# Separate PSUM tiles for the narrow channel group, and layer-norm statistics in three TensorE passes, in a Swin block with a dynamic convolution

## The chip, the cores and the metric

The kernel runs on one NeuronCore of a Trainium2 chip (trn2). The metric is device time in microseconds of one execution, the median of several. The engines are named as in the profile: PE (TensorE) multiplies, PEld loads its weights, DVE (VectorE) and ACT (ScalarE) work on vectors, POOL (GpSimd) works in this kernel on data in SBUF, SP issues transfers. In this kernel PSUM, in banks, holds the results of TensorE; a PSUM tile is what the program allocates there at once, one bank or two. All runs told of here are fast ones; a program on one core shows no second state in these runs.

## The reference, cut to what matters

The input is (16, 192, 56, 56) in f32. One shifted-window attention block (7x7 windows, 6 heads), its MLP, and then a depthwise convolution whose weights depend on the image's pooled result:

```python
h = _ln(transpose(x), norm1_g, norm1_b)          # over 192 channels
...                                              # roll, windows, attention
x1 = shortcut + transpose(h)
y = _ln(transpose(x1), norm2_g, norm2_b)         # over 192 channels
y = gelu(y @ fc1_w + fc1_b) @ fc2_w + fc2_b      # 192 -> 768 -> 192
x = x1 + transpose(y)
pooled = x.mean(axis=(2, 3))                     # "taps": weights per image and channel
wt = (relu(bn(pooled @ w1.T)) @ w2.T + b2) * MASK
out = depthwise_conv(x, wt) + bias
```

## The kernel before

192 channels are a wide group of 128 and a narrow group of 64. A step handles two rows of windows, 2 x 392 tokens; four steps make an image, 64 steps the batch. The wide group lies on 128 partitions with the two token halves side by side; the narrow group has its two halves one above the other, on partitions 0-63 and 64-127. Each step of the loop carries the MLP of step i-2, the attention of step i, the value and query products of step i+1, the norm-1 statistics of step i+2 and the norm-2 statistics of step i-1, and pieces of an older image's convolution. PSUM is cut into four pairs of banks, called A, B_, C, D in the loop; a pair is one tile.

The statistics are sums over channels of x and of x squared, made by TensorE with a 32-column constant, so that each result lands on one strip of 32 partitions:

```python
def norm_squares(key, i, side, engine):          # engine: ACT for norm 2, GpSimd for norm 1
    ...                                          # s0 = squares of the wide group, s1 of the narrow one
    sqs[key] = s0, s1

def norm_stats(key, i, side):                    # called once for each side
    v0, v1 = flat_of(i)
    s0, s1 = sqs.pop(key)
    st = bank(side)
    for k in range(2):
        for h in range(2):
            for at, u0, u1 in ((side * 64, v0, v1), ((1 - side) * 64, s0, s1)):
                lhs, rhs = (sel[:, 0], u0[:, h]) if k == 0 else (sel[:, 1 + h], u1)
                p = at + h * 32
                mm(st[p : p + 32, :T], lhs, rhs, k == 0, k == 1)
```

The second half of a step, with the two banks of one pair C shared by three narrow results:

```python
singles[0] = banks(f"s_{i}", C)                  # one PSUM tile of two banks
o = attention_rows(i, attention_values(i, prts, D))   # wide into D, narrow into bank(1); ACT copies out
mlp_narrow(hid, bank(0))                         # narrow part of the second MLP product
for c in ys:
    conv_rest(*c)                                # DVE: three taps of a convolution piece
mlp_out(i - 2, 1, bank(0)[:, :T])                # DVE reads bank(0)
pp, pp1, p_narrow, p_rest, p_whole = project(i, o, A)  # wide into A, narrow into bank(1)
p_narrow(); p_rest()
pvs, v_rest, v_whole = attention_v(i + 1, (B_, D))
v_rest()
if (i - 2) % STEPS == STEPS - 1:                 # every fourth step
    convs.append({... "wt": taps(b, taps_pool(b))})    # a small matmul into bank(0), DVE work
p_whole()
residual(i, pp, pp1)                             # DVE
v_whole()
attention_v_out(pvs)                             # DVE and ACT copy the values out
norm_squares(f"2_{i}", i, 1, nc.scalar)          # ACT
```

(Cut: conditions that only matter at the ends of the loop.)

Of the kernel before, what the change touches and what calls it, by code (L numbers as in the profile page):

```python
# [10 lines left out]
ALU = mybir.AluOpType  # L11
# [25 lines left out]
def tile_swin_then_dynamic_conv(  # L37
# [45 lines left out]
    def banks(name, k):  # L83
        return psum.tile([128, 2, 512], F32, tag=f"pair{k}", name=name)
# [3 lines left out]
    def bank(k):  # L88
        return singles[0][:, k]

    def mm(dst, lhs, rhs, start, stop):
        nc.tensor.matmul(dst, lhs, rhs, start=start, stop=stop, skip_group_check=True)  # L92
# [134 lines left out]
    def flat_of(i):  # L227
        v0, v1 = rows_of(i)
        return v0.rearrange("p h r c -> p h (r c)"), v1.rearrange("p r c -> p (r c)")
# [8 lines left out]
    def norm_squares(key, i, side, engine):  # L238
        v0, v1 = flat_of(i)
        s0 = one.tile([128, 2, T], F32, tag=f"sq0{side}", name=f"sq0_{key}")  # L240
        s1 = one.tile([128, T], F32, tag=f"sq1{side}", name=f"sq1_{key}")
        if engine is nc.scalar:
            nc.scalar.activation(s0, v0, AF.Square)
            nc.scalar.activation(s1, v1, AF.Square)
        else:
            engine.tensor_tensor(s0, v0, v0, ALU.mult)
            engine.tensor_tensor(s1, v1, v1, ALU.mult)
        sqs[key] = s0, s1

    def norm_stats(key, i, side):  # L250


        v0, v1 = flat_of(i)
        s0, s1 = sqs.pop(key)
        st = bank(side)
        for k in range(2):
            for h in range(2):
                for at, u0, u1 in ((side * 64, v0, v1), ((1 - side) * 64, s0, s1)):
                    lhs, rhs = (sel[:, 0], u0[:, h]) if k == 0 else (sel[:, 1 + h], u1)
                    p = at + h * 32  # L260
                    mm(st[p : p + 32, :T], lhs, rhs, k == 0, k == 1)
        stats[side] = st

    def norm_vars(keys):

# [243 lines left out]
    def attention_weigh(po, po1, wp, prt):  # L509
        for s in range(2):  # L510
            w = wp * 2 + s
            for a, g in ((0, 0), (0, 1), (1, 0), (1, 1), (0, 2), (1, 2)):

                r, k = (g, a) if g < 2 else (a, 2)
                o = po[:, a] if g < 2 else po1
                at = (g if g < 2 else a) * 64
                mm(
                    o[at : at + 64, w * N : (w + 1) * N],
                    vbd[:, a, w, g, :],
                    prt[:, r, k * PW + s * 64 : k * PW + s * 64 + N],  # L520
                    True,
                    True,
                )

    def attention_values(i, prts, k):

        po = banks(f"po_{i}", k)
        for wp in range(4):
            attention_weigh(po, bank(1), wp, prts[wp])
        return po[:, 0], po[:, 1], bank(1)  # L530

    def attention_rows(i, pos):

# [5 lines left out]
            )  # L539
        return o.rearrange("p k r w c -> p k (r w c)")  # L540

    def project(i, o, k):

        pp = banks(f"pp_{i}", k)
        pp1 = bank(1)

        def narrow():
            for a in range(2):
                mm(pp1[a * 64 : a * 64 + 64, :T], wp0[:, C0:DIM], o[:, a], True, False)

        def rest():
            for a in range(2):
                p = slice(a * 64, a * 64 + 64)
                mm(pp[:, a, :T], wp1[p], o[p, 2], True, False)

        def whole():
            mm(pp1[:, :T], wp2, o[:, 2], False, True)
            for a in range(2):
                mm(pp[:, a, :T], wp0[:, 0:C0], o[:, a], False, True)

        return pp, pp1, narrow, rest, whole
# [39 lines left out]
            long(dsts[f], wf1, cols(f), y0, False)  # L601
            gelu(f)

    def mlp_narrow(hid, pf1):
        for f in range(NFC):
            for a in range(2):
                mm(
                    pf1[a * 64 : a * 64 + 64, :T],
                    wf2[:, f, C0:DIM],
                    hid[:, f, a],  # L610
                    f == 0,
                    f == NFC - 1,
                )

    def mlp_wide(i, hid, k, turn):
        pf = banks(f"pf_{i}", k)
# [8 lines left out]
    def mlp_out(i, c, p):  # L625

        b, s = divmod(i, STEPS)
        if b not in sums:
            sums[b] = small.tile([128, 2, STEPS], F32, tag="sums", name=f"sums_{b}")
        v = flat_of(i)[c]  # L630
        nc.vector.scalar_tensor_tensor(
            v, p, f2b[c], v, ALU.add, ALU.add, accum_out=sums[b][:, c, s : s + 1]
        )
# [8 lines left out]
        nc.vector.tensor_copy(x1[64:128, 0, :], x1[0:64, HALF, :])  # L642
        return pooled

    def taps(b, pooled):

        pt = bank(0)
        for kc in range(2):
            mm(pt[:, 0:RED], pooled[:, kc].broadcast_to([128, 128]), w1t[:, kc], kc == 0, kc == 1)
        tt = small.tile([128, 1, RED], F32, tag="tt", name=f"tt_{b}", bufs=1)  # L650
        nc.vector.tensor_tensor(tt[:, 0], pt[:, 0:RED], bn[:, 0], ALU.mult)
        nc.vector.tensor_tensor(tt[:, 0], tt[:, 0], bn[:, 1], ALU.add)
        tw = small.tile([128, 2 * NTAP, RED], F32, tag="tw", name=f"tw_{b}", bufs=1)
        nc.vector.scalar_tensor_tensor(
            tw,
            tt.broadcast_to([128, 2 * NTAP, RED]),
            0.0,
            w2n.rearrange("p k t r -> p (k t) r"),
            ALU.max,
            ALU.mult,  # L660
        )
        wt = small.tile([128, 2, NTAP], F32, tag="wt", name=f"wt_{b}")
        nc.vector.tensor_reduce(
            wt.rearrange("p k (t o) -> p (k t) o", o=1), tw, AX.X, ALU.add
        )
        nc.vector.tensor_tensor(wt, wt, b2t, ALU.add)
        return wt
# [51 lines left out]
    def has(i):  # L719
        return 0 <= i < NS  # L720
# [11 lines left out]
        return ready  # L732

    def stats_of(i):
        keys = {}
        if has(i + 2):
            keys[0] = f"1_{i + 2}"
            norm_stats(keys[0], i + 2, 0)
        if has(i - 1):
            keys[1] = f"2_{i - 1}"  # L740
            norm_stats(keys[1], i - 1, 1)
        return keys

    def tail_of(i, o, kp, kv):

        pvs, v_rest, v_whole = attention_v(i + 1, kv) if has(i + 1) else (None, None, None)
        if o is not None:
            pp, pp1, narrow, rest, whole = project(i, o, kp)
            narrow()
            rest()  # L750
        if pvs:
            v_rest()
        if o is not None:
            whole()
            residual(i, pp, pp1)
        if pvs:
            v_whole()
            attention_v_out(pvs)
        if o is not None:
            norm_squares(f"2_{i}", i, 1, nc.scalar)  # L760
# [178 lines left out]
    for i, extra in ((0, (proj_bias, mlp_weights)), (1, (taps_weights,))):  # L939
        top, share = attention_scores(i, *qs.pop(i), (1, 2, 0, 1))  # L940
        norm1_scale(i + 1, dvs.pop(0), nc.gpsimd)
        top(0)
        for wp in range(3):
            top(wp + 1)
            share(wp)
        share(3)
        qs[i + 1], outs = attention_qk(i + 1, 1, 0, 2)
        for f in outs:
            f()
        for e in extra:  # L950
            e()
        keys = stats_of(i)
        dev = norm_devs(keys)
        dvs.update(norm_spread(keys, dev))
        prts = [attention_turn(i, wp, wp % 2) for wp in range(4)]
        if 1 in keys:
            yns[i - 1] = norm2_scale(i - 1, dvs.pop(1))
        norm_squares(f"1_{i + 3}", i + 3, 0, nc.gpsimd)
        o = attention_rows(i, attention_values(i, prts, 0))
        tail_of(i, o, 1, (2, 0))  # L960


# [3 lines left out]
    for i in range(2, NS + 2):  # L966
# [67 lines left out]
            yns[i - 1] = norm2_scale(i - 1, dvs.pop(1))  # L1034
        if has(i + 3):
            norm_squares(f"1_{i + 3}", i + 3, 0, nc.gpsimd)
        singles[0] = banks(f"s_{i}", C)
        if has(i):
            o = attention_rows(i, attention_values(i, prts, D))
        mlp_narrow(hid, bank(0))  # L1040
        for c in ys:
            conv_rest(*c)
        mlp_out(i - 2, 1, bank(0)[:, :T])
        if has(i):
            pp, pp1, p_narrow, p_rest, p_whole = project(i, o, A)
            p_narrow()
            p_rest()
        if has(i + 1):
            pvs, v_rest, v_whole = attention_v(i + 1, (B_, D))
            v_rest()  # L1050
        if (i - 2) % STEPS == STEPS - 1:
            b = (i - 2) // STEPS
            convs.append({"b": b, "n": 0, "wt": taps(b, taps_pool(b))})
        if has(i):
            p_whole()
            residual(i, pp, pp1)
        if has(i + 1):
            v_whole()
            attention_v_out(pvs)
        if has(i):  # L1060
            norm_squares(f"2_{i}", i, 1, nc.scalar)
        pairs = [C, A, B_, D]
    c = convs.pop()
    for n in range(6):
        conv_rest(c["b"], c["wt"], n, conv_begin(c["b"], c["wt"], n))
# [74 lines left out]
```

## Time and profile before

| | before |
|---|---|
| median time | 3428.9 us (3428.0 to 3432.4, three runs) |
| TensorE busy | 93% |
| period of a normal step, start of the statistics to the next | 51.06 us |
| period of a step with taps, every fourth | 51.85 us |
| statistics matmuls of one step | 2.84 us |
| granted TensorE clock, 300 to 3000 us | 1.00 |

The periods are the distance between the first statistics matmuls of successive steps in the timeline of TensorE. From the fifth on, all but one repeat within 0.05 us, which makes them a far finer ruler than the total. The length of the statistics is given either to the modelled end of the last matmul (2.84 us before, 2.18 after) or to the start of the next product (2.77 and 2.11). The rows of the page, of the waits and of the timeline are shown in the prediction. In a row of the timeline the bracket is the idle time before an instruction and what ended it; in a row of the waits the three numbers are the total, the count and the longest.

### The profile page before, as it was taken

The numbers are of one execution on the slowest core, as the hardware profiler recorded it, in microseconds if no ns is written. First come the engines' busy times: TensorE is split into PE (matmuls) and PEld (weight loads), VectorE is DVE, ScalarE is ACT, GpSimd is POOL, SyncE is SP. The second block draws the span as 40 slices with busy tenths as digits, with TensorE's granted clock in tenths as the row PEclk, the third lists the DMA queues.
The fourth block names the chain that finished last, engine by engine and source line by source line (L and its number), as shares of the span: only waits on it lengthen the run. The fifth ranks groups of instructions, "written<-read, shape, count | busy, mean of one in ns | idle before, by whom it ended". The sixth has DMA issues, their size and how long they took to land.

```text
span 3430.2 us, 64894 instructions
## 1 busy us (share of the span) xinstructions
PE 3183.9 (93%) x26642; PEld 1955.5 (57%) x26642; DVE 2078.5 (61%) x3893; ACT 1854.5 (54%) x2988; POOL 759.8 (22%) x656
## 2 busy tenths in 40 slices
PE   5799999999999999999999999999999999999996
PEld 3455555555555555555555555555555555555553
DVE  4354675665665665665665666665665656666564
ACT  3354564565565565565565565565565565555552
POOL 4211212212212212212212212212212222222220
PEclk7799999999999999999999999999999999999998
DMA  3101102111111102101111201102111110201001
GB/s 94 19 10 48 29 25 57 34 48 34 51 27 38 53 26 61 29 27 55 34 51 31 59 23 35 53 29 58 29 30 52 34 54 28 62 22 32 25 29 43
DMA packets 79124, 135.39 MB, mean 39 GB/s; under 512 B 21766, under 2 KB 61692, under 8 KB 76908
## 3 DMA queue, kind: packets, MB, share of 16 engines
q1 hardware_dynamic: 77266, 128.54, 13.3%
q8 instruction: 210, 3.44, 0.4%
q0 software_dynamic: 1056, 1.92, 0.3%
q10 hardware_dynamic: 506, 0.79, 0.1%
q14 instruction: 86, 0.70, 0.1%
HBM read 41.25 MB, written 38.54 MB: 23 GB/s over the span
## 4 chain that ended last, share of the span: by engine, by line
PE 84%; ACT 7%; DVE 4%; issue 1%; POOL 0%; DMA 0%; SPq 0%; DVEq 0%; POOLq 0%; ACTq 0%
PE ph L92 23%; PE pf L92 15%; PE s L92 10%; PE pv L92 7%; PE st L92 5%; PE pq L92 4%; PE pp L92 4%; PE sc L92 4%; PE pe L92 4%; PE pk L92 4%; PE pt L500 3%; ACT o L536 2%; ACT prt L506 2%; ACT L235 2%; DVE y L688 2%
## 5 line engine op out<-in xcount | busy, mean ns | idle before, releaser
L92 PE MATMUL ph<-yn,wf 128*128 128x392 f32 (+1 forms) x3072 | 802.3, 498 | 6.1 <-ACT vbd L443 3.3
L487 POOL TENSOR_TENSOR prob<-e,tot 113x588 f32<-113x588 f32 x256 | 297.8, 1174 | 1966.6 <-DVE tot L486 1966.6
L92 PEld LDWEIGHTS ph<-yn,wf 128*128 128x128 f32 (+1 forms) x3072 | 429.4, 189 | 350.6 <-issue 87.2
L443 ACT COPY vbd<-pv 49x192 f32<-49x192 f32 x512 | 135.4, 312 | 888.7 <-DVE vbd L441 888.5
L92 PE MATMUL pf<-hid,wf 128*128 128x392 f32 x1536 | 538.3, 494 | 3.5 <-ACT hid L588 2.0
L688 DVE SCALAR_TENSOR_TENSOR y<-x,wt,y 128x770 f32<-128x770 f32 x288 | 328.1, 1141 | 288.1 <-ACT y L673 281.4
L588 ACT ACTIVATE hid<-ph,f1b 128x784 f32<-128x784 f32 x384 | 336.8, 912 | 137.7 <-PE ph L92 137.7
L92 PEld LDWEIGHTS pf<-hid,wf 128*128 128x128 f32 x1536 | 281.5, 190 | 183.7 <-ACT hid L588 3.3
L92 PE MATMUL s<-hid,wf 128*64 128x392 f32 x1536 | 266.9, 496 | 88.6 <-ACT o L536 88.6
L92 PEld LDWEIGHTS pv<-wqkv,win 64*128 64x128 f32 (+1 forms) x2048 | 259.7, 190 | 39.6 <-ACT kbd L393 2.8
L471 DVE TENSOR_TENSOR e<-sc,bias_t 113x588 f32<-113x588 f32 x256 | 179.5, 761 | 168.0 <-PE sc L92 167.8
L92 PE MATMUL pv<-wqkv,win 64*128 64x192 f32 (+1 forms) x2048 | 274.0, 327 | 3.3 <-ACT kbd L393 2.5
L478 DVE TENSOR_TENSOR e<-e,top 113x588 f32<-113x588 f32 x256 | 266.5, 1041 | 8.9
L338 POOL TENSOR_TENSOR yn<-x,dv 128x784 f32<-128x784 f32 x64 | 132.0, 2063 | 565.4 <-DMA dv<-dev 537.8
L235 ACT ACT_TABLE_LOAD x192 | 246.3, 1283 | 3.4
L506 ACT COPY prt<-pt 128x678 f32<-128x678 f32 x256 | 179.1, 726 | 117.5 <-PE pt L500 116.0
L481 ACT ACTIVATE e<-e 113x588 f32<-113x588 f32 x256 | 176.8, 691 | 108.7 <-DVE e L478 108.7
L92 PEld LDWEIGHTS s<-hid,wf 128*64 128x64 f32 x1536 | 104.5, 137 | 216.2 <-issue 119.9
L441 DVE COPY vbd<-pv 49x192 f32<-49x192 f32 x512 | 159.1, 349 | 97.0 <-ACT vbd L443 83.0
L500 PEld LDWEIGHTS pt<-ident,prob 113*128 113x128 f32 x1536 | 167.3, 142 | 74.4 <-issue 45.3
L500 PE MATMUL pt<-ident,prob 113*128 113x113 f32 x1536 | 182.7, 262 | 10.3 <-ACT prt L506 8.5
L92 PE MATMUL po<-prt,vbd 128*64 128x49 f32 x4096 | 191.5, 225 | 0.2 <-ACT prt L506 0.2
(157 smaller groups left out, 4688.9 us busy)
## 6 DMA issues: line engine op xcount, KB each, us to landing
dv<-dev SPq DMA_DIRECT2D x1020, 49.0 KB
x<-in_x_dram SPq DMA_DIRECT2D x15, 1484.0 KB
out_dram<-y SPq DMA_DIRECT2D x48, 392.0 KB
out_dram<-y SPq DMA_DIRECT2D x48, 196.0 KB
x<-in_x_dram SPq DMA_DIRECT2D x16, 392.0 KB
x<-in_x_dram SPq DMA_DIRECT2D x15, 350.0 KB
out_dram<-y SPq DMA_DIRECT2D x16, 308.0 KB
out_dram<-y SPq DMA_DIRECT2D x16, 154.0 KB
```

The costliest lines, as they stand in the source:

```text
L92: nc.tensor.matmul(dst, lhs, rhs, start=start, stop=stop, skip_group_check=True)
L235: nc.scalar.activation(junk, eps_t[0:1], func)
L441: nc.vector.tensor_copy(dst, f)
L443: nc.scalar.copy(dst, f)
L471: nc.vector.tensor_tensor(e, sc[:PW, :, : HEADS * N], rel, ALU.add)
L478: nc.vector.tensor_tensor(ehs[wp], ehs[wp], t.broadcast_to([PW, 2 * HEADS, N]), ALU.subtract)
L481: nc.scalar.activation(es[wp], es[wp], AF.Exp)
L487: nc.gpsimd.tensor_tensor(prob[wp][:PW, :, 0:N], ehs[wp], t.broadcast_to([PW, 2 * HEADS, N]), ALU.mult)
L500: nc.tensor.transpose(pt[:, a, g * PW : (g + 1) * PW], prob[wp][:PW, h : h + 2, :].rearrange("p h k -> p (h k)"), ident[:PW, :PW],)
L506: nc.scalar.copy(prt, pt[:, :, : 3 * PW])
L588: nc.scalar.activation(hid[:, f], phs[f][:, :, :T], AF.Gelu, bias=f1b[:, f : f + 1])
L688: nc.vector.scalar_tensor_tensor(dst, src, wt[:, kc, t : t + 1], dst, ALU.mult, ALU.add)
```

## The change

It has two aims. First, three statistics passes instead of four: the squares of the narrow group are added to those of the wide group on GpSimd, so that one pass over the sum does what two did, and both sides are run together to keep all four strips of 32 columns full. Second, each narrow result gets a PSUM tile of its own, which needs another turn of the pairs, and the taps move behind the rest of the projection and values to find a free pair.

```diff
+        for h in range(2):
+            p = slice(h * 64, h * 64 + 64)
+            nc.gpsimd.tensor_tensor(s0[p, h], s0[p, h], s1[p], ALU.add)
+        sqs[key] = s0
...
+        for k in range(3):
+            for side in keys:
+                v0, v1 = flat_of(steps[side])
+                for h in range(2):
+                    p = (side if k < 2 else 1 - side) * 64 + h * 32
+                    dst = stats[side][p : p + 32, :T]
+                    if k == 0:
+                        mm(dst, sel[:, 0], v0[:, h], True, False)
+                    elif k == 1:
+                        mm(dst, sel[:, 1 + h], v1, False, True)
+                    else:
+                        mm(dst, sel[:, 0], sqs[keys[side]][:, h], True, True)
...
-        singles[0] = banks(f"s_{i}", C)
-            o = attention_rows(i, attention_values(i, prts, D))
-        mlp_narrow(hid, bank(0))
+            o = attention_rows(i, attention_values(i, prts, D, C))
+        pf1 = mlp_narrow(i - 2, hid, A)
...
-            pp, pp1, p_narrow, p_rest, p_whole = project(i, o, A)
+            pp, pp1, p_narrow, p_rest, p_whole = project(i, o, B_, C)
-            pvs, v_rest, v_whole = attention_v(i + 1, (B_, D))
+            pvs, v_rest, v_whole = attention_v(i + 1, (D, A))
             v_rest()
-        if (i - 2) % STEPS == STEPS - 1:
-            convs.append({"b": b, "n": 0, "wt": taps(b, taps_pool(b))})
             p_whole()
             residual(i, pp, pp1)
             v_whole()
+        if (i - 2) % STEPS == STEPS - 1:
+            convs.append({"b": b, "n": 0, "wt": taps(b, taps_pool(b), C)})
             attention_v_out(pvs)
...
-        pairs = [C, A, B_, D]
+        pairs = [C, B_, D, A]
```

(Cut: the first two steps, the signatures, conditions that only matter at the ends.)

More of the change, by code (lines that the diff above doesn't have):

```diff
@@ L247, in norm_squares, with norm_stats @@
             engine.tensor_tensor(s1, v1, v1, ALU.mult)
-        sqs[key] = s0, s1
-    def norm_stats(key, i, side):
-        v0, v1 = flat_of(i)
-        s0, s1 = sqs.pop(key)
-        st = bank(side)
-        for k in range(2):
-            for h in range(2):
-                for at, u0, u1 in ((side * 64, v0, v1), ((1 - side) * 64, s0, s1)):
-                    lhs, rhs = (sel[:, 0], u0[:, h]) if k == 0 else (sel[:, 1 + h], u1)
-                    p = at + h * 32
-                    mm(st[p : p + 32, :T], lhs, rhs, k == 0, k == 1)
-        stats[side] = st
+        for h in range(2):
+            p = slice(h * 64, h * 64 + 64)
+            nc.gpsimd.tensor_tensor(s0[p, h], s0[p, h], s1[p], ALU.add)
+        sqs[key] = s0
+    def norm_stats(keys, steps):
+        for side in keys:
+            stats[side] = bank(side)
+        for k in range(3):
+            for side in keys:
+                v0, v1 = flat_of(steps[side])
[8 more added lines that the diff above has]
+                        mm(dst, sel[:, 0], sqs[keys[side]][:, h], True, True)
+        for side in keys:
+            sqs.pop(keys[side])
     def norm_vars(keys):
@@ L523, in attention_weigh, with attention_values @@
                 )
-    def attention_values(i, prts, k):
-        po = banks(f"po_{i}", k)
+    def attention_values(i, prts, k, k1):
+        po, po1 = banks(f"po_{i}", k), banks(f"po1_{i}", k1)[:, 0]
         for wp in range(4):
-            attention_weigh(po, bank(1), wp, prts[wp])
-        return po[:, 0], po[:, 1], bank(1)
+            attention_weigh(po, po1, wp, prts[wp])
+        return po[:, 0], po[:, 1], po1
     def attention_rows(i, pos):
@@ L540, in attention_rows, with project @@
         return o.rearrange("p k r w c -> p k (r w c)")
-    def project(i, o, k):
-        pp = banks(f"pp_{i}", k)
-        pp1 = bank(1)
+    def project(i, o, k, k1):
+        pp, pp1 = banks(f"pp_{i}", k), banks(f"pp1_{i}", k1)[:, 0]
         def narrow():
@@ L602, in mlp_first, with mlp_narrow @@
             gelu(f)
-    def mlp_narrow(hid, pf1):
+    def mlp_narrow(i, hid, k):
+        pf1 = banks(f"pf1_{i}", k)[:, 0]
         for f in range(NFC):
@@ L613, in mlp_narrow @@
                 )
+        return pf1
     def mlp_wide(i, hid, k, turn):
@@ L643, in taps_pool, with taps @@
         return pooled
-    def taps(b, pooled):
-        pt = bank(0)
+    def taps(b, pooled, k):
+        pt = banks(f"t_{b}", k)[:, 0]
         for kc in range(2):
@@ L734, in stats_of @@
     def stats_of(i):
-        keys = {}
-        if has(i + 2):
-            keys[0] = f"1_{i + 2}"
-            norm_stats(keys[0], i + 2, 0)
-        if has(i - 1):
-            keys[1] = f"2_{i - 1}"
-            norm_stats(keys[1], i - 1, 1)
+        steps = {side: k for side, k in ((0, i + 2), (1, i - 1)) if has(k)}
+        keys = {side: f"{side + 1}_{k}" for side, k in steps.items()}
+        norm_stats(keys, steps)
         return keys
@@ L747, in tail_of @@
         if o is not None:
-            pp, pp1, narrow, rest, whole = project(i, o, kp)
+            pp, pp1, narrow, rest, whole = project(i, o, kp, 3)
             narrow()
@@ L949, in tile_swin_then_dynamic_conv @@
             f()
+        if i:
+            singles[0] = banks("singles", 3)
         for e in extra:
@@ L958, in tile_swin_then_dynamic_conv @@
         norm_squares(f"1_{i + 3}", i + 3, 0, nc.gpsimd)
-        o = attention_rows(i, attention_values(i, prts, 0))
+        o = attention_rows(i, attention_values(i, prts, 0, 3))
+        singles[0] = None
         tail_of(i, o, 1, (2, 0))
@@ L1036, in tile_swin_then_dynamic_conv @@
             norm_squares(f"1_{i + 3}", i + 3, 0, nc.gpsimd)
-        singles[0] = banks(f"s_{i}", C)
         if has(i):
-            o = attention_rows(i, attention_values(i, prts, D))
-        mlp_narrow(hid, bank(0))
+            o = attention_rows(i, attention_values(i, prts, D, C))
+        pf1 = mlp_narrow(i - 2, hid, A)
         for c in ys:
             conv_rest(*c)
-        mlp_out(i - 2, 1, bank(0)[:, :T])
+        mlp_out(i - 2, 1, pf1[:, :T])
         if has(i):
-            pp, pp1, p_narrow, p_rest, p_whole = project(i, o, A)
+            pp, pp1, p_narrow, p_rest, p_whole = project(i, o, B_, C)
             p_narrow()
@@ L1048, in tile_swin_then_dynamic_conv @@
         if has(i + 1):
-            pvs, v_rest, v_whole = attention_v(i + 1, (B_, D))
+            pvs, v_rest, v_whole = attention_v(i + 1, (D, A))
             v_rest()
-        if (i - 2) % STEPS == STEPS - 1:
-            b = (i - 2) // STEPS
-            convs.append({"b": b, "n": 0, "wt": taps(b, taps_pool(b))})
         if has(i):
@@ L1058, in tile_swin_then_dynamic_conv @@
             v_whole()
+        if (i - 2) % STEPS == STEPS - 1:
+            b = (i - 2) // STEPS
+            convs.append({"b": b, "n": 0, "wt": taps(b, taps_pool(b), C)})
+        if has(i + 1):
             attention_v_out(pvs)
```

## The prediction

> **What bounds the kernel now.** I read the page first (busy times and the clock row), then the list of waits, then one step in order of time on each engine. The page says that TensorE is busy for 93% of the span, and no other engine for more than 61%:
>
> ```profile
> PE 3183.9 (93%) x26642; PEld 1955.5 (57%) x26642; DVE 2078.5 (61%) x3893; ACT 1854.5 (54%) x2988; POOL 759.8 (22%) x656
> PE 84%; ACT 7%; DVE 4%; issue 1%; POOL 0%; DMA 0%; SPq 0%; DVEq 0%; POOLq 0%; ACTq 0%
> ```
>
> So the reader should see a TensorE-bound kernel in which ACT and DVE own 11% of the chain that ended last. The granted clock is 1.00 in every stretch from 200 to 3300 us, and only the first 200 us run at 0.72 to 0.84. The list of waits for TensorE names two that come once in each of 62 steps; the columns after the colon are us in total, times, and the longest:
>
> ```profile
> PE s L92 <- ACT o L536: 88.6, 62, 1.5
> PE s L92 <- DVE x L631: 52.2, 62, 1.2
> ```
>
> Every other row of that list is a start-up event or under 9 us. The timeline of TensorE inside a normal step (one that also runs two convolution pieces) shows where the two sit; columns are start, length, what, and in brackets the idle time before it:
>
> ```profile
> 1649.30 4.17 PE L92 MATMUL s<-hid,wf 128*64 128x392 f32 x24 [1.48 <-ACT o L536]
> 1654.28 0.88 PE L92 MATMUL s<-o,wp 128*64 128x392 f32 x4 [0.81 <-DVE x L631]
> ```
>
> The narrow MLP product (tile s, bank 0) waits until ACT has copied the attention output out of s, bank 1, although it neither reads that output nor writes that bank. Then the narrow projection (s, bank 1) waits until DVE has read the MLP result out of bank 0. Both are waits between two halves of one PSUM tile. Without a convolution piece in front of the copies the first one is 1.31 us.
>
> The statistics matmuls in the same timeline come in groups of four starting within 0.03 us of each other, one group every 0.33 us:
>
> ```profile
> 1670.12 0.52 PE L92 MATMUL st<-x,sel 128*32 128x392 f32 x1
> 1670.13 0.52 PE L92 MATMUL st<-sq,sel 128*32 128x392 f32 x1
> 1670.13 0.52 PE L92 MATMUL st<-x,sel 128*32 128x392 f32 x1
> 1670.14 0.52 PE L92 MATMUL st<-sq,sel 128*32 128x392 f32 x1
> 1670.47 0.49 PE L92 MATMUL st<-x,sel 128*32 128x392 f32 x1
> ...
> 1672.89 0.60 PE L92 MATMUL ph<-yn,wf 128*128 128x392 f32 x1
> ```
>
> One pass over four column strips is two such groups (each f32 matmul leaves two records); four passes are eight groups, 1670.12 to 1672.89 = 2.77 us with the change-over. From the starts of these statistics I get the period: 51.04 to 51.09 us for a normal step and 51.85 us for every fourth step, the one that works out the convolution taps.
>
> **What the Trainium skill says.** (1) TensorEngine Tiling (Array Packing), Tiling Modes: a 128x32 configuration gives four tiles that run independently. The trace agrees, by the four starts above. So passes count, not matmuls: with the four strips full, a pass removed is worth two groups. (2) PSUM — Partial Sum Buffer, The four PSUM rules: accumulation groups in different quadrants of one bank are independent. The new order leaves mean and variance groups open side by side in different quadrants, so it should be correct; no time follows from it. (3) SBUF — State Buffer, Who interferes with whom: a DVE instruction with two SBUF inputs contends with a GpSimd instruction that reads SBUF, and the second one blocks. The trace agrees: the DVE subtraction at 1681.42 takes 0.77 us, the same one at 1685.27, beside a GpSimd product, 1.31 us. (4) Perfetto Trace Analysis, GPSIMD Engine Instruction, calls GpSimd spans unreliable and advises start-to-start spacing; I use the merged pair of 64x392 products, 2.10 us for two.
>
> **The change, part by part.**
>
> Statistics: three passes for four. Two groups go, 2 x 0.325 = 0.65 us of a TensorE that has no slack there. Per step: -0.65.
>
> The narrow MLP product gets its own PSUM pair, A. A's last reader is the ACT copy of the fourth transposed block, which ends at 1645.62; the product can start when the attention values end, about 1647.8. The 1.48 us go (1.31 in a taps step). The idle figure is counted from a modelled end; elsewhere in the timeline a successor starts 0.15 us before its predecessor's modelled end, so I add that: -1.63 (-1.46).
>
> The narrow projection goes to pair C. It needs ACT's copies of o, which end at 1649.25, while the MLP product then runs to about 1652: hidden. The 0.81 us go, again with 0.1 of overlap: -0.9.
>
> The value projection's second block now sits in A and must wait for DVE to read the MLP result. In a normal step that DVE read starts as the product ends and takes 0.63 us, while TensorE has 0.8 + 0.75 + 0.65 us of other matmuls. But in the two of three convolution steps whose later piece has the extra row fix, DVE is in that piece until 1704.62 and reads until 1705.3; by my count TensorE wants A at 1705.05. +0.3 in two of three: +0.2.
>
> GpSimd gains four additions of 64x392 per step, 4 x 1.05 = 4.2 us; in all 256 x 1.1 = 280 us, 22% to about 31% busy. The pair for norm 1 follows the squares that end at 1657.4 and is not needed until 1670. The pair for norm 2 starts when ACT's squares end at 1666.53, ends by about 1668.9 even with some blocking by DVE's scaling, and is needed by the third pass at 1670.12 + 1.31 = 1671.4. Slack 2.5 us: hidden.
>
> Normal step: 51.06 - 0.65 - 1.63 - 0.9 + 0.2 = 48.1 us.
>
> The taps step is where something is given back. Before, the taps ran ahead of the residual, in DVE's free time; the diff puts them behind the residual and ahead of the copies of the value projection. Their DVE rows:
>
> ```profile
> 1602.27 0.16 DVE L638 TENSOR_REDUCE pooled<-sums 128x2 f32<-128x8 f32 x1
> 1602.46 1.18 DVE L641 COPY x<-x 64x56 f32<-64x56 f32 x1
> 1603.65 0.78 DVE L642 COPY x<-x 64x56 f32<-64x56 f32 x1
> 1605.94 0.21 DVE L651 TENSOR_TENSOR tt<-s,bn 128x48 f32<-128x48 f32 x1 [1.50 <-PE s L92]
> 1606.18 0.21 DVE L652 TENSOR_TENSOR tt<-tt,bn 128x48 f32<-128x48 f32 x1
> 1606.42 0.56 DVE L654 SCALAR_TENSOR_TENSOR tw<-tt,w2n 128x384 f32<-128x384 f32 x1
> 1607.02 0.55 DVE L663 TENSOR_REDUCE wt<-tw 128x8 f32<-128x384 f32 x1
> 1607.61 0.17 DVE L666 TENSOR_TENSOR wt<-wt,b2t 128x8 f32<-128x8 f32 x1
> ```
>
> Take the end of the narrow MLP product as zero. The normal step puts the end of the residual at +6.65 and the end of the value projection on TensorE at +7.5. The taps matmul (0.45 us of stream) follows at +7.6, but DVE reads its result only after the two copies, at +8.9 to +9.1. The next MLP product wants the same pair C, so it waits about 0.9 us. DVE finishes the taps at +10.75, and the DVE and ACT copies of the first value block end 2.45 us later, at +13.2. TensorE wants that bank at 9.0 + 2 x 1.3 = +11.6: a wait of 1.6 us. The ACT squares and first three Gelus shift likewise, and the statistics wait some 0.6 us for the third Gelu. Sum: taps step = 51.85 - 0.95 (old taps matmul and its wait) - 0.65 - 1.46 - 0.9 + 0.45 + 0.9 + 1.6 + 0.6 = 51.4 us. It gains next to nothing.
>
> Start-up: the additions delay the first statistics by about 2 us and lengthen the GpSimd queue there; the passes give some back. +4 us. Step 63, outside the sixty periods counted, gains 3.
>
> Sum: 45 x (51.06 - 48.1) + 15 x (51.85 - 51.4) = 133 + 7 = 140; 3429 - 140 - 3 + 4 = 3290 us.
>
> **The rivals.** (a) The taps waits don't happen, because the copies run shorter or TensorE is later than I count. Then 15 x 3.1 = 47 us more go: 3243. The timeline's copies averaged 1.64 us together for 1.96 in the step shown, which speaks for a little of it; the order of DVE's instructions speaks against it. (b) A second bound takes over once TensorE is 2.9 us earlier: the broadcast of the deviations by DMA, then the GpSimd scaling that feeds the next step's first matmul. That scaling ends 14.9 us before the statistics at the latest while the MLP starts 8.2 before, so 6.7 us of slack become 4. I don't expect it; were it so, 2 us a step would be lost and the time would be 3400. (c) GpSimd's additions come late and the third pass waits, or they block DVE's scaling long enough to hold up the copies. One late pair of 2.2 us per step would make 3420. The slack of 2.5 us speaks against it. (d) The new matmul order fills the strips worse, and the statistics stay at 2.7 us: 3330. The old order with alternating sources already packs, and the strips still rotate through all four.
>
> **Range and chances.** All the removed waits are in the trace with nearly the same size in each step, so most of the error is the taps step (0 to -47 us) and unforeseen waits (0.7 us a step would be +42). I take 3290, with 3250 to 3335 for 8 in 10. The 2% line is at 3360; to miss it, half the gain must fail. Faster 0.93, same 0.06, slower 0.01.
>
> **What would show it.** The two rows for s gone from TensorE's waits; the statistics 2.1 us long; normal period 48.1; four-step cycle with one step of about 51.4, in which the MLP matmuls wait for DVE's tt and then for ACT's or DVE's vbd; GpSimd at 30%, with no wait of TensorE for sq. A wait of st for sq, of ph for yn, or of pv for x in most steps would prove me wrong, as would a lower granted clock.

## The result, and the profile after

The changed kernel takes 3256.8 us (median of four, 3253.5 to 3261.5), against 3428.5 us for the kernel before in the same rounds. The ratio is 0.950, with a 95% interval of 0.948 to 0.951. Here and below a ratio is the mean time of one kernel's fast runs over that of the other's of the same rounds, so it is not quite the ratio of the two medians. The prediction said 3290 us, with 3250 to 3335 as its range: right, and 33 us on the slow side.

The page of the changed kernel, busy times and the chain that ended last by engine:

```profile
PE 3128.8 (96%) x26130; PEld 1938.8 (59%) x26130; DVE 2155.5 (66%) x3893; ACT 1855.1 (57%) x2988; POOL 1020.4 (31%) x912
PE 89%; DVE 4%; ACT 2%; issue 1%; POOL 0%; DMA 0%; ACTq 0%; DVEq 0%; POOLq 0%
```

ACT's share of the chain falls from 7% to 2%, and TensorE is busy for 96%. TensorE now has 512 records fewer; DVE has the same instructions as before and yet 77 us more busy time. The waits of TensorE that come once or more per image (total, times, longest):

```profile
PE ph L92 <- ACT vbd L452: 18.8, 16, 3.3
...
PE ph L92 <- DVE tt L661: 5.9, 15, 0.4
PE pv L92 <- DVE x L641: 4.4, 11, 0.5
```

The two rows of 62 waits each are gone. What is left are the two waits of the taps steps and a small one in 11 steps. The timeline of TensorE in a normal step shows the narrow MLP product (called pf here, 64 columns) and the narrow projection (pp) following each other with no bracket, and the statistics in three passes (16 records for x, 8 for the summed squares):

```profile
989.65 4.13 PE L92 MATMUL pf<-hid,wf 128*64 128x392 f32 x24
993.62 1.69 PE L92 MATMUL pp<-o,wp 128*64 128x392 f32 x8
...
1009.41 1.52 PE L92 MATMUL st<-x,sel 128*32 128x392 f32 x16
1010.75 0.84 PE L92 MATMUL st<-sq,sel 128*32 128x392 f32 x8
1011.52 0.93 PE L92 MATMUL ph<-yn,wf 128*128 128x392 f32 x2
```

From 1009.41 to the next product is 2.11 us where it was 2.77. The period of an undisturbed normal step is 47.68 us, that of a taps step 50.14 us. A taps step on TensorE, then on DVE:

```profile
1144.84 0.54 PE L92 MATMUL t<-w1t,pooled 128*128 128x48 f32 x4
1145.77 2.87 PE L92 MATMUL ph<-yn,wf 128*128 128x392 f32 x8 [0.39 <-DVE tt L661]
1149.67 5.90 PE L92 MATMUL ph<-yn,wf 128*128 128x392 f32 x28 [1.03 <-ACT vbd L452]
```

```profile
1143.95 1.04 DVE L651 COPY x<-x 64x56 f32<-64x56 f32 x1
1145.01 0.18 DVE L652 COPY x<-x 64x56 f32<-64x56 f32 x1
1145.42 0.21 DVE L661 TENSOR_TENSOR tt<-t,bn 128x48 f32<-128x48 f32 x1 [0.23 <-PE t L92]
```

The first MLP product waits for DVE to read the taps result out of its pair, and the next piece of it for the copies of the first value block, which DVE starts only when the taps are done. Both waits were forecast; both are shorter than forecast. The second row copy takes 0.18 us here, where the same copy took 0.78 us in the step of the kernel before that the prediction shows; GpSimd's additions had ended at 1144.95. The copies end before the taps matmul does: the bracket says that DVE waited 0.23 us for the matmul (t), and it waits so in all 16 taps of this trace, 10.4 us in total.

The balance over the 59 whole periods that both traces hold: from 3025.2 us (before: 3259.46 - 234.30) to 2857.7 us (after: 3094.24 - 236.53), 167.5 us less. Of these, 15 taps steps give 15 x (51.85 - 50.14) = 26 us and 44 normal steps the other 142. The spans differ by 170.5 us, so start and end together give 3.

### The profile page after: what moved, and what is told of

The parts are those of the page before. It is cut to its first block, busy times and chain, and to the rows that moved or that the text cites. A ratio compares the mean times of both kernels' runs of the same rounds, so it can differ in the third digit from the quotient of the medians.

```text
span 3259.7 us, 64143 instructions
## 1 busy us (share of the span) xinstructions
PE 3128.8 (96%) x26130; PEld 1938.8 (59%) x26130; DVE 2155.5 (66%) x3893; ACT 1855.1 (57%) x2988; POOL 1020.4 (31%) x912
## 4 chain that ended last, share of the span: by engine, by line
PE 89%; DVE 4%; ACT 2%; issue 1%; POOL 0%; DMA 0%; ACTq 0%; DVEq 0%; POOLq 0%
PE ph L92 23%; PE pf L92 22%; PE pv L92 7%; PE pp L92 7%; PE po L92 5%; PE pq L92 4%; PE pt L509 4%; PE sc L92 4%; PE st L92 4%; PE pe L92 4%; PE pk L92 4%; DVE y L698 1%; DVE vbd L450 1%; DVE y L707 1%; ACT vbd L452 1%
## 5 line engine op out<-in xcount | busy, mean ns | idle before, releaser
L92 PE MATMUL ph<-yn,wf 128*128 128x392 f32 (+1 forms) x3072 | 811.4, 501 | 27.3 <-ACT vbd L452 18.8
L92 PE MATMUL pf<-hid,wf 128*128 128x392 f32 (+1 forms) x3072 | 802.8, 494 | 3.5 <-ACT hid L596 2.0
L92 PEld LDWEIGHTS pf<-hid,wf 128*128 128x128 f32 (+1 forms) x3072 | 386.4, 164 | 303.6 <-issue 119.9
L698 DVE SCALAR_TENSOR_TENSOR y<-x,wt,y 128x770 f32<-128x770 f32 x288 | 321.0, 1116 | 214.8 <-ACT y L683 208.1
L250 POOL TENSOR_TENSOR sq<-sq,sq 64x392 f32<-64x392 f32 x256 | 262.9, 1027 | 383.1 <-ACT sq L244 368.6
L641 DVE SCALAR_TENSOR_TENSOR x<-pf,cols,x 128x784 f32<-128x784 f32 (+1 forms) x128 | 105.8, 827 | 232.8 <-PE pf L92 225.7
L92 PE MATMUL pp<-o,wp 128*128 128x392 f32 (+2 forms) x896 | 253.0, 517 | 2.6 <-ACT o L545 2.6
L92 PE MATMUL po<-prt,vbd 128*64 128x49 f32 x6144 | 199.9, 225 | 0.2 <-ACT prt L515 0.2
```

Source lines behind the costliest of these rows:

```text
L92: nc.tensor.matmul(dst, lhs, rhs, start=start, stop=stop, skip_group_check=True)
L250: nc.gpsimd.tensor_tensor(s0[p, h], s0[p, h], s1[p], ALU.add)
L698: nc.vector.scalar_tensor_tensor(dst, src, wt[:, kc, t : t + 1], dst, ALU.mult, ALU.add)
```

## The experiments

The theory was: TensorE sets the end; the waits between halves of a PSUM tile and the fourth pass are separate losses that add up; the additions are hidden; and DVE's place for the taps gives a part back. The rivals: one part carries everything; the additions cost time through the third pass or by blocking DVE; the waits were of the data or the bank, not of the tile. Thirteen kernels ran, the changed one among them. The kernel before was timed beside them in each call, at 3426.7 to 3430.9 us, so I compare ratios to it; an experiment's microseconds can be set against 3257 within about 3 us.

### 1. Only the tiles separated

The changed kernel with norm_squares, norm_stats and their caller as before.

```diff
-            nc.gpsimd.tensor_tensor(s0[p, h], s0[p, h], s1[p], ALU.add)
-        for k in range(3): ...
+        for k in range(2): ...        # as before, once for each side
```

> The changed kernel with the old statistics: four passes of eight matmuls per side pair, no additions on GpSimd; only the PSUM tiles are separated. Theory (the two waits between halves of one tile carry most of the gain, the third pass is 0.65 us a step that nothing hides): 60 x 0.65 = 39 us slower than the changed kernel, less about 2 us of start-up that the additions cost, so 3257 + 37 = 3294 us, normal period 48.3 us, statistics 2.83 us long. Rival (the passes were hidden behind the waits before and the tiles carry everything): 3257 us. Rival (the tiles carry little and the statistics unlock the rest): above 3340 us.

Measured: 3292.6 us, ratio 0.960 (0.959 to 0.961). Normal period 48.33 us, taps step 50.80 us, statistics 2.84 us. The tiles alone give 4.0%. The fourth pass costs 48.33 - 47.68 = 0.65 us in each step, to the hundredth what two groups of four matmuls were worth.

### 2. Only the three passes

The kernel before with the new statistics and additions.

> The kernel before with the three statistics passes and the additions on GpSimd, PSUM tiles as before. Theory: the gain adds up, 39 us less than before plus 2 us of start-up: 3391 us, both waits of the narrow tile still there at 1.3 to 1.5 and 0.8 us in 62 steps. Rival (the waits for ACT and DVE swallow the saved pass, since those engines set the step): 3428 us.

Measured: 3396.4 us, ratio 0.990 (0.989 to 0.992). Normal period about 50.42 us, and the two old waits are there with their old totals:

```profile
PE s L92 <- ACT o L545: 88.5, 62, 1.5
PE s L92 <- DVE x L640: 52.7, 62, 1.2
```

1.0% here (clear of the noise, though under 2%) and 4.0% in the first experiment make the 5.0% of both. The parts add, so neither wait hid the pass, and neither ACT nor DVE set the step. The rival with 3428 us falls.

### 3. One tile for two narrow results

The narrow MLP product and the narrow projection go back into the two banks of one tile; all else keeps its own.

```diff
-        pf1 = banks(f"pf1_{i}", k)[:, 0]
+        both = banks(f"pf1_{i}", k)
+        pf1, other = both[:, 0], both[:, 1]
-            pp, pp1, p_narrow, p_rest, p_whole = project(i, o, B_, C)
+            pp, pp1, p_narrow, p_rest, p_whole = project(i, o, B_, C, other)   # pp1 = other
-            pvs, v_rest, v_whole = attention_v(i + 1, (D, A))
+            pvs, v_rest, v_whole = attention_v(i + 1, (D, C))
```

(Cut: the taps go to A, and the pairs turn as A, B_, D, C.)

> The changed kernel with the MLP's narrow product and the narrow projection put back into the two banks of one PSUM tile (the attention output and the taps keep their own; the second value block takes the pair that falls free). Theory (a wait comes from the tile, not from the bank or the data): the wait of the narrow projection for DVE's read of the MLP result is back, 0.8 us in normal steps with a plain convolution piece and taps steps, up to 1.6 us where the piece has a row fix, the wait of the value projection for that read gone: 3257 + about 68 = 3325 us. Rival (waits are kept per bank, and what held the projection before was something else): 3257 us or less.

Measured: 3374.9 us (3366.0 to 3385.4), ratio 0.984. The wait is back in 62 steps: 88.5 us in total, up to 2.7. The banks differ and the data are unrelated, so the tile is what makes it wait. This is shown for the second of the two old waits; the first, of the narrow MLP product for ACT's copy, is removed in experiment 1 but was not brought back alone, so for it the tile as the cause is argued by analogy. The shared tile cost 118 us where I expected 68. The timeline and the granted clock around one of the long waits, TensorE first (then, for windows of the span: busy times of the five engines, granted clock, DMA share, GB/s):

```profile
1467.77 1.57 PE L92 MATMUL pf<-o,wp 128*64 128x392 f32 x4 [2.63 <-DVE x L643]
...
1470.74 2.77 PE L92 MATMUL pv<-wqkv,win 64*128 64x192 f32 x16
```

```profile
1466.00:1472.00 6.00, 4.23 (x16) 2.42 (x18) 1.62 (x3) 0.00 (x0) 5.69 (x6) 0.60 0.30 95
1472.00:1478.00 6.00, 6.00 (x30) 4.63 (x29) 2.68 (x8) 0.00 (x0) 0.48 (x1) 0.83 0.00 0
```

After the wait the sixteen value matmuls take 2.77 us instead of 1.47, and the granted clock is 0.60 and then 0.83, where it was 1.00 from 1461 to 1466 us. Some of the long waits are followed by a lower clock. I looked at the ten microseconds after each such wait from 400 to 3250 us: a clock of 0.68 to 0.85 follows 6 waits, of 2.0 to 2.7 us, and none of the shorter ones; but six other waits of 2.6 us keep 1.00, and so does one of 2.1. What decides it these runs do not show. The clock that those six windows lack comes to some 12 us, an estimate of what it cost (10 us each, five at 0.83 to 0.85 and one at 0.68). The TensorE page of the Trainium skill (TensorE: Matmul & The Clock Gate, HAM oscillation) warns of idle gaps above about 3.4 us; these traces, which decide, show the drop after shorter ones, now and then.

The other part is the waits themselves: 1.43 us on average (88.5 / 62) where the expected 68 us come to about 1.26 a step (60 x 1.26, less 8 us for the wait of the value projection that goes). A row copy in the fourth and sixth convolution piece makes DVE late there. This was tested next.

### 4 and 5. Without the row copy

The changed kernel, and the one-tile kernel, without that copy. One row of each image comes out wrong, on purpose.

```diff
-        if n in (3, 5):
+        if False:
             ...
             nc.vector.tensor_copy(y[p, LAST - 3 * PR, :], cbk[p].broadcast_to(...))
```

> The changed kernel without DVE's copy that mends one row in the fourth and sixth convolution piece (a wrong result in those rows on purpose). Theory (the 0.33 to 0.50 us that the value projection waits for DVE in 11 steps come from that copy, which the GpSimd scaling blocks for up to 1.7 us when the broadcast lands at the wrong moment): those waits are gone and every normal step is 47.7 us, 8 us less, 3249 us. Rival (DVE's order or the position of the step, not the copy): 3257 us, waits still there.

Measured: 3251.5 us, ratio 0.948 (0.947 to 0.949), 5 us less by the medians and 6 by the ratio, whose interval overlaps that of the changed kernel; the periods are the evidence. The wait of pv for DVE is gone from the list, and all 44 normal periods are 47.67 or 47.68 us. This explains the 11 steps of 48.3 to 48.45 us in the changed kernel. DVE and GpSimd in one of them, changed kernel:

```profile
1037.78 2.08 DVE L698 SCALAR_TENSOR_TENSOR y<-x,wt,y 128x770 f32<-128x770 f32 x2 [3.30 <-ACT y L683]
1039.89 1.74 DVE L707 COPY y<-cols 128x56 f32<-128x56 f32 x1
```

```profile
1039.55 2.03 POOL L347 TENSOR_TENSOR yn<-x,dv 128x784 f32<-128x784 f32 x1 [8.03 <-DMA dv<-dev]
```

The transfer landed just before the row copy, GpSimd took its product first, and a copy that takes 0.19 us when it has the way to itself ended only after GpSimd's product, 1.74 us later (in this trace 21 of the 32 row copies take 0.19 to 0.20 us, and 11 take 1.73 to 1.90; those 11 lie in the 11 long steps, one in each).

> The kernel with the MLP's narrow product and the narrow projection in one PSUM tile, again without the row copy (wrong rows on purpose). Theory (the 50 us that this kernel lost beyond what was expected are the longer wait in steps with a row copy, 1.6 to 2.7 us, and the lower granted clock that followed some of those waits): all waits of the projection for DVE are 0.8 to 0.9 us, the granted clock stays at 1.00, and the time is that of the changed kernel without the row copy plus 60 x (0.9 + 0.15) = 63 us, 3312 us. Rival (the shared tile costs something that the copy has no part in): above 3340 us.

Measured: 3331.2 us (3327.6 to 3337.0), ratio 0.972. This lies between the theory and its rival. The waits sum to 69.5 us for 88.5; most are 0.83 to 0.9 us as expected, but eighteen of those from 400 to 3250 us are still 1.6 to 1.8 us, and the clock drops after two. The shared tile costs 80 us without the row copy (3331.2 - 3251.5) and 118 with it, where 63 and 68 were expected. So the row copy carries most of the excess (it falls from 50 to 17 us), and the expectation that all waits would be short was wrong. In one of the long ones the three ordinary taps of a convolution piece take 4.74 us beside GpSimd's product, instead of 3.13: that collision alone makes a wait of 1.74 us.

### 6. No additions

> The changed kernel without the additions on GpSimd (the variance misses the last 64 channels: a wrong result on purpose). Theory (the additions are hidden in every step and cost only at the start): 2 to 3 us less, 3254 us, normal period 47.7 us as in the changed kernel. Rival (the additions hold up DVE through the shared port, or the third pass waits for them): 15 us less or more, 3242 us or under, and a shorter period.

```diff
-            nc.gpsimd.tensor_tensor(s0[p, h], s0[p, h], s1[p], ALU.add)
```

Measured: 3251.8 us, ratio 0.948 (0.946 to 0.949): 5 us less, between the theory's 3 and the rival's 15, and hardly more than the noise (the intervals overlap). The periods tell where: undisturbed normal steps are 47.68 us and taps steps 50.16 us, the same as with the additions. The sixth statistics start at 229.4 us and not at 236.5; in the traces of experiments 4 and 9 to 12, whose start is that of the changed kernel, they begin at 232.5 to 236.1. The additions cost 3 to 7 us at the start and nothing that the periods show after it. They do slow DVE; these are its groups of the norm-1 scaling, in the kernel before and in the changed one (busy us, mean ns, idle before):

```profile
L327 DVE TENSOR_TENSOR win<-x,dv 64x28 f32<-64x28 f32 x124 | 22.3, 180 | 0.9
L319 DVE TENSOR_TENSOR win<-x,dv 128x21 f32<-128x21 f32 x124 | 16.9, 179 | 0.9
```

```profile
L336 DVE TENSOR_TENSOR win<-x,dv 64x28 f32<-64x28 f32 x124 | 72.9, 588 | 0.9
L328 DVE TENSOR_TENSOR win<-x,dv 128x21 f32<-128x21 f32 x124 | 61.3, 534 | 0.9
```

95 us more of DVE "busy" are DVE blocked by the two additions. Without them the means are back at 180 ns. With the shorter span it explains the higher share of DVE on the page (the busy time of before, 2078.5 us, would be 64% of the new span), and it costs nothing, because DVE waits for ACT right after it anyway: in the normal steps that I looked at this wait shrank from 2.83 us to 1.26. The waits of TensorE in the taps steps are the same without the additions (5.9 us for tt, 18.8 for vbd).

### 7 and 8. The norm-2 additions twice and three times

```diff
-        for h in range(2):
+        for h in [0, 1] * (2 if side else 1):      # and 3
```

> The changed kernel with the two additions for the second norm done twice (a wrong result on purpose). Theory (they are hidden with a slack of some 2.6 us before the third statistics pass, of which they would use 2.2 more; in taps steps the slack is about 1.7 us): next to nothing, 15 x 0.5 = 7 us, 3264 us. Rival (each addition costs on its own): 2.2 us a step, 3257 + 130 = 3390 us.

Measured: 3265.2 us, ratio 0.952 (0.951 to 0.953), as forecast. The statistics that follow a taps step are 2.66 to 2.69 us long instead of 2.18, the half microsecond expected; the others stay at 2.18.

> The changed kernel with the two additions for the second norm done three times (a wrong result on purpose). Theory (slack 2.6 us in normal and 1.7 us in taps steps, 4.3 us more work): the third pass waits 1.7 us in a normal and 2.6 us in a taps step, 45 x 1.7 + 15 x 2.6 = 115 us more, 3372 us, shown as waits of st for GpSimd's sq. Rival (the additions have slack of a whole step, or the wait is absorbed further on): under 3290 us.

Measured: 3443.3 us, ratio 1.004. The wait is of the kind forecast and larger: 186 us more than the changed kernel, not 115. A normal step, TensorE, then GpSimd:

```profile
1311.30 0.83 PE L92 MATMUL st<-sq,sel 128*32 128x392 f32 x4
1312.52 0.85 PE L92 MATMUL st<-sq,sel 128*32 128x392 f32 x2 [0.39 <-POOL sq L250]
1314.21 0.85 PE L92 MATMUL st<-sq,sel 128*32 128x392 f32 x2 [0.84 <-POOL sq L250]
```

```profile
1306.43 7.73 POOL L250 TENSOR_TENSOR sq<-sq,sq 64x392 f32<-64x392 f32 x6 [4.10 <-ACT sq L244]
```

Six additions take 7.73 us for my 6.5, because they now run into the three taps of a convolution piece on DVE, which take 4.69 us for 3.13: each blocks the other. The third pass also falls apart into three pieces of two or four records. The last matmul starts when the last addition ends, 2.9 us late in this step. Where no convolution piece runs beside them the statistics are 3.9 us long, 1.7 us late as I had worked out; after a taps step they are 3.9 us late for my 2.6. So the slack of the additions is real, and in a normal step it is about one pair wide.

### 9 to 12. The place of the taps

Four variants of the changed kernel. In the first the result of the taps matmul goes to the pair of the second MLP product. In the second DVE's taps work is cut in two around the copies of the value projection. The third does both. The fourth puts the taps back ahead of the residual, in the second bank of the narrow projection's tile, which nobody used.

```diff
# 9
-            taps(b, taps_pool(b), C)
+            taps(b, taps_pool(b), B_)
# 10: pooled sum and first product, then the value copies, then the rest
+            tt = taps(b, taps_pool(b), C)
         attention_v_out(pvs)
+            taps_rows(b)
+            convs.append({... "wt": taps_finish(b, tt)})
# 12
+            pt = p_other                 # second bank of the tile of pp1
+            convs.append({... "wt": taps(b, taps_pool(b), pt)})
         p_whole()
         residual(i, pp, pp1)
```

> The changed kernel with the taps matmul's result in the pair of the wide projection (needed by the second MLP product) in place of the pair that the first MLP product needs. Theory (in a taps step TensorE waits in the end for the copies of the first value block, whose time DVE sets): the wait for tt of 0.39 us goes, the wait for vbd grows from 1.03 to 1.42 us, the period of a taps step stays 50.1 us and the time 3257 us. Rival (the two waits add): 15 x 0.39 = 6 us less, 3251 us.

Measured: 3258.6 us, ratio 0.950 (0.949 to 0.951), no gain. The wait for tt is gone and that for vbd has grown from 18.8 to 27.2 us in 16 times; taps step 50.14 us. Here a wait that ends before another one on the same engine was not worth its own length.

> The changed kernel with DVE's work for the taps cut: only the pooled sum and the first product stay ahead of the copies of the value projection, the row copies and the other four instructions go behind them. Theory: the copies start 1.5 us earlier, the wait for vbd of 1.03 us goes and that for tt of 0.39 stays; 15 x 1.03 = 15 us less, 3241 us, taps step 49.1 us. Rival (something else follows at once, such as the Gelu that the statistics wait for): 3250 us or more.

Measured: 3239.9 us, ratio 0.945 (0.944 to 0.946); taps step 48.68 us, the following step 47.90. The wait for vbd is gone in the loop, that for tt stays (5.9 us in 15 times). A taps step and its successor gain 1.24 us together, 0.2 more than the wait; why was not tested.

> Both edits together: DVE's taps work cut as described, and the taps matmul's result in the pair of the wide projection. Theory: neither wait is left, 15 x 1.42 = 21 us less than the changed kernel, 3236 us, taps step 48.7 us. Rival as for the cut alone.

Measured: 3237.6 us, ratio 0.944 (0.943 to 0.946); taps step 48.51 us. But the following step is 48.07 us, with a new wait of the scores for DVE of 0.3 us in 15 steps. The two periods together are 96.58 us, as with the first edit alone: what the second edit adds is given back there, and the 2 us between the two medians are within the noise.

> The changed kernel with the taps back in their old place, ahead of the whole-width part of the projection, in the unused second bank of the narrow projection's tile. Theory (what the taps step lost is due to the place of DVE's work in its order): the waits for tt and vbd in the MLP go, a wait of about 0.5 us for tt ahead of the projection comes; 14 us less, 3243 us, taps step about 49.2 us. Rival (the old place costs as much because the residual and the copies then start later): 3257 us.

Measured: 3237.2 us (3235.4 to 3238.9), ratio 0.944 (0.943 to 0.945); taps step 48.62 us in 8 of 15 and up to 49.23 in the others. TensorE waits once for tt, in the projection:

```profile
1131.55 2.24 PE L92 MATMUL pp<-o,wp 128*128 128x392 f32 x6 [0.30 <-DVE tt L661]
```

Three of the four beat both kernels, with right results. They are not apart from each other beyond the noise. The fourth is the simplest: DVE starts its taps work in time that it idles away in the changed kernel (2.96 us ahead of the residual), and shares the projection's tile at the price of 0.3 us. It is 5.6% faster than the kernel before, and the place of the taps was worth 20 us that the change gave away.

## Why the prediction was right

It forecast the time within 33 us of a change of 172. The waits of the shared tile, the pass and the hidden additions came as described; two terms, both about copies by DVE, had the mechanism wrong. Term by term:

| term | predicted | measured | where |
|---|---|---|---|
| fourth pass, per step | -0.65 us | -0.65 us | normal period, experiment 1 to changed kernel |
| both waits of the shared tile, normal step | -2.53 us | -2.73 us | 51.06 - 48.33, experiment 1 |
| value projection behind DVE, mean | +0.2 us | +0.17 us (0.67 in 11 of 44) | periods of the changed kernel |
| normal step, mean | 48.1 us | 47.85 us | periods |
| taps: wait for tt | 0.9 us | 0.39 us | waits |
| taps: wait for vbd | 1.6 us | 1.03 us | waits |
| taps: statistics behind the Gelu | 0.6 us | 0 | timeline |
| taps step | 51.4 us | 50.14 us | periods |
| additions in the steps | 0 | 0 | experiment 6 |
| start-up | +4 us | +2.2 us, not clear of the spread between traces | sixth statistics at 236.5 for 234.3 |

The largest part of the 33 us is the taps step: 1.26 us in 15 steps, 19 us. The step of the prediction that failed there is that DVE reads the taps result "only after the two copies". It put this read at +8.9 to +9.1 us after the narrow MLP product. In the trace above the copies end at +7.8, and DVE reads at +8.0, as soon as the taps matmul ends; it waits for that matmul in all 16 taps, so the copies are on the path in none of them. Experiment 6 agrees: both copies take 0.18 us there, and the two waits and the period are unchanged. The prediction had taken the copies' 1.18 and 0.78 us from a step in which GpSimd was busy, although it named the contention and even the mean of 1.64 us; in the changed kernel they take 0.76 us together on average, and 1.22 at most. DVE's chain thus starts about 1 us earlier than forecast, both waits are shorter, and the third does not appear. The other terms of that step's sum came out some 0.4 us larger, the other way; why is open.

The value projection's +0.2 us is right on average by luck. The prediction had 0.3 us in each step with the row copy, two of three convolution steps; measured is 0.67 us in 11 of 44 and nothing in the others. It had read DVE's lateness off a step (at 1699 us) in which the row copy takes 1.72 us, while 22 of the 32 row copies in that trace take 0.19 to 0.20. Not the copy but its collision with GpSimd's product makes DVE late, as experiment 4 shows.

Three small slips change nothing: in that step DVE's next instruction starts at 1704.67 and not 1704.62, the granted clock is below 1.00 in the last 130 us too (0.89), and 2 us a step in rival (b) would make 3410 and not 3400.

The second part of the 33 us is the normal step, 0.25 us in 44, 11 us: removing two waits gave 0.2 us more than the idle time plus the 0.25 us of overlap that I had allowed for. What that overlap consists of was not tested.

Of the rivals, (a) happened in part: the copies did run shorter, and the taps waits are 1.4 us rather than none. For (b), GpSimd's scaling ends 11.7 us before the statistics at the latest, 3.5 us before the MLP needs it: slack fell from 6.7 us but did not run out, and nothing waits for it but one product at the very end, for 2.3 us. For (c), the slack of the third pass is shown by experiments 7 and 8, and blocked DVE scaling is real and harmless. For (d), the strips are as full as before.

## What to carry to other kernels

Two results that share a PSUM tile wait for each other's readers even when they lie in different banks; if a matmul waits for a copy of something that it doesn't use, give it its own tile, and check what the new turn of the pairs makes the next user wait for. When work moves to another place in an engine's order, price it by what runs beside it there, not by its old duration, ask whether it ends last, and follow the engine's later work to the next buffer that somebody waits for. Where two waits follow each other on an engine, the later end can be what counts: removing the first alone gained nothing here.

## What the Trainium skill lacked or had wrong

- No page has it: a wait kept per PSUM tile, not per bank. Between unrelated halves of one tile it cost 1.31 to 1.48 and 0.8 us a step before, and 0.83 to 2.7 us when it was brought back in experiment 3.
- TensorE: Matmul & The Clock Gate, HAM oscillation, warns of idle gaps of more than about 3.4 us. Here a lower granted clock followed 6 waits of 2.0 to 2.7 us in one trace (down to 0.60 in a window of 6 us) and two of 1.8 us in another, while six more of 2.6 us kept 1.00. In experiment 8 one drop followed waits of 1.35 and 0.84 us (0.83 over ten microseconds).
- TensorEngine Tiling (Array Packing), Tiling Modes, gives the independence of the four 32-column tiles, with which the traces agree (four starts within 0.03 us), but not what becomes of a pass whose operands come apart: in experiment 8 two strips of the third pass ran alone, two records each at 1312.52 and 1314.21 us, each when its addition had ended.
- SBUF — State Buffer, Who interferes with whom, states that DVE and GpSimd block each other on the shared port, and the traces agree. It does not say how this looks in a profile, where the blocked time is inside the instruction's duration: DVE's 64x28 product shows a mean of 588 ns beside GpSimd's additions and 180 ns without, so busy time can rise with no more work done (by 77 us here).
